# Taking the transposes of the large segments off TensorE in a fused Mamba-2 and feed-forward kernel

## The chip, the cores and the metric

The kernel runs as one program on one core of one Trainium2 chip. The metric is the time of one execution on the device, in microseconds (us). Smaller is better. The figure for a kernel is the median of its timed runs. Beside the timed runs there is one profiled execution, from which all durations of single instructions come.

## The reference, cut to what matters

The input `u` has 4 sequences of 1024 tokens with 256 features, in float32. One layer is computed: a Mamba-2 mixer, then a feed-forward block with 4-bit weights, each with a layer norm on its input, a layer norm on its output and a residual.

```python
x = u                                                    # (4, 1024, 256)
x = x + layernorm(mamba2(layernorm(x)))
x = x + layernorm(ffn(layernorm(x)))

def mamba2(u):
    z, xBC, dt = split(u @ in_proj)                      # 512 | 512+128+128 | 8
    xBC = silu(causal_conv1d(xBC))                       # 4 taps along the tokens
    x, B, C = split(xBC)                                 # 8 heads of 64 | 128 | 128
    dt = softplus(dt + dt_bias)
    # scan over the tokens of state[h] = exp(dt*A) * state[h] + B (x*dt), y = C . state + D*x
    y = scan(x, dt, A, B, C, D) * silu(z)
    y = y * rsqrt(mean(y*y) + EPS) * norm_weight
    return y @ out_proj                                  # 512 -> 256

def ffn(x):                                              # weights from 4-bit codes and block scales
    return (gelu(x @ Wg.T) * (x @ Wu.T)) @ Wd.T          # 256 -> 2048 -> 256
```

## The kernel before, in words

The 4096 tokens are cut into nine segments (`SEGS`): the first half of sequence 0 as two segments of 256 tokens (segments 0 and 1), and seven "large" segments of 512 tokens (segments 2 to 8). A large segment has four token blocks of 128. For every segment there is a mixer part (`mixer(s)`) and a feed-forward part (`ffn(s)`).

Matrix products contract over the partitions, so activations have to stand with features on the partitions ("by feature") for one product and with tokens on the partitions ("by token") for another. The kernel turns a tile with TensorE: a transpose is a product with the constant `ident`, 128 columns at a time, into a bank of PSUM, and ScalarE or VectorE then reads that bank. There are three such places:

- `norm_in`: the mixer's input `x` is normalised by token into `xn` (VectorE) and turned into `xnT` (two transposes for a token block, then a ScalarE copy for each half of the features).
- `inner(i)`: after the convolution, `xc` stands by feature. For each token block its four feature tiles of x are turned into the bank `px`, which VectorE reads twice (for `xdt` and `xw`), and the feature tile of B is turned into `pgb` and copied by ScalarE to `bt`. Five transposes for a token block.
- `turned(i)`: the normalised input of the feed-forward part, `xf`, is turned into `xfT`. Two transposes for a token block and one ScalarE copy.

The steps of a mixer are in this order: `norm_in`, `step_sizes` (dt), `features` and `convolve` for the six feature tiles, `decays`, then for the token blocks `inner`, `scan`, `gated`, `way_out` and `turned`, each a step behind the one before. From segment 4 on (`SEVEN`) and in the feed-forward of all large segments, a 2x2 block product is done with seven products instead of eight (`pair`, `seven`); the weights for it are fetched from DRAM (`stock`, `mstock`) into `wide` and `win` by SyncE's queue, and VectorE and ScalarE do additions and copies between the products. `widen_pair(j)` makes two of the 16 tiles of the hidden layer, and `narrow` multiplies by the last weight matrix into the banks `d`.

The program does not issue instructions as it is written. A `Recorder` takes down every instruction with its inputs, outputs and buffers, and `issue` then plays a list schedule: for each engine it picks, among what could start soonest, the step of lowest `rank`, and takes over the order found. A mixer of segment s has rank 10s - 10, the products of the feed-forward of segment s rank 25 + 10s and its last product rank 27 + 10s. So a mixer goes ahead of the feed-forward three segments before it. Costs of the plan are in `weigh`; for a DMA, `issue` takes 60 ns on SyncE's queue, then the bytes by a rate on one shared wire and 1700 ns to landing, and lets a consumer on another engine start `LATE_DMA` = 1500 ns after that. Each engine, SyncE's DMA queue among them, then runs its list strictly in order and waits where an input is not there. All instructions have the same line in the profile (L379, the place where the plan is written out), so they are told apart by tile names: `xn`, `xc` and `xf` with `ident` are transposes, `f` and `a` and `d` are banks of PSUM.

Buffers are handed out in the order of the recording, too. There are three `x`, two `xfT`, two `xf`, three `th`, one `xnT`, one `xc`, and two banks `a`. `big[0]` and `big[1]` hold the hidden layer of segments 0 and 1; later `big[0]` holds that of the large segments, and `big[1]` the gelu values of `widen_pair`.

Of the kernel before, what the change touches and what calls it, by code (L numbers as in the profile page):

```python
# [17 lines left out]
P = 128  # L18
# [18 lines left out]
SIDE = 2  # L37
OUT = True
SEVEN = 4
MASKED = -2.0 ** 100  # L40

ATANH = (2.000000007877749, 0.6666631593507933, 0.400248537235466, 0.2796141883358907,
# [126 lines left out]
class Recorder:  # L169
# [118 lines left out]
    def issue(self, tc, rank, patience):  # L288


        steps = self.steps
        follows = [[] for _ in steps]
        for st in steps:
            st.missing = len(st.before)
            st.ready = st.floor
            st.rank = rank(st)
            for b in st.before:
                follows[b.at].append(st)
        open_ = {e: [] for e in self.ENGINES.values()}
        table = "exp"  # L300
        for st in steps:
            if not st.missing:
                open_[st.engine].append(st)
        free = {e: 0.0 for e in open_}
        wires = 0.0
        bundle = None
        order = []
        while len(order) < len(steps):
            best = None
            for e, sts in open_.items():  # L310
                when = {}
                for st in sts:
                    starts = [b.pool.may_start(b) for b in st.buffers]
                    if None not in starts:
                        when[st] = max(starts + [st.ready, free[e]])
                if e == "ACT" and when:


                    now = min(when.values())
                    other = [st for st in when if st.table not in (None, table)]  # L320
                    for st in other:
                        when[st] += SWITCH
                    if len(other) < len(when):
# [12 lines left out]
            t, st = best  # L336
            e = st.engine
            st.start = t
            if e == "ACT" and st.table:
                table = st.table  # L340
            turn = min(PORT, max(0.0, free["POOL"] - t)) if st.port and t < EARLY else 0.0
            free[e] = t + st.busy + turn
            st.end = free[e] + st.after
            if st.name == "dma_start":
                if st.bytes > 20000:
                    wires = max(free[e], wires) + st.bytes / (230.0 if st.repeats else 350.0)
                    st.end = wires + 1700.0
# [12 lines left out]
            order.append(st)  # L360
            for f in follows[st.at]:
                flows = f.before[st]
                if e == "PE" and f.engine == "PE":
                    r = st.start
                elif f.engine != e:
                    r = st.end + slack(e, f.engine)
                elif flows:
                    r = st.end
                else:
                    r = st.start  # L370
                f.ready = max(f.ready, r)
                f.missing -= 1
                if not f.missing:
                    open_[f.engine].append(f)
        self.order = order
        with tc.manual_schedule():
            for st in order:
                real = lambda a: a.on(a.buf.pool.slots[a.buf.slot]) if isinstance(a, View) else a
                getattr(getattr(self.nc, st.queue), st.name)(  # L379
                    *[real(a) for a in st.args], **{k: real(a) for k, a in st.kwargs.items()})  # L380
# [25 lines left out]
def mamba_ffn_kernel(  # L406
    ctx: ExitStack,
    tc: tile.TileContext,
    u: bass.AP,
    w_in: bass.AP,  # L410
    conv_w: bass.AP,
    conv_b: bass.AP,
# [25 lines left out]
    def given(ap):  # L438
        return Pool([ap]).get()

    u, w_in, conv_w, conv_b, dt_bias, a_log, d_skip, norm_w, w_out = map(
        given, (u, w_in, conv_w, conv_b, dt_bias, a_log, d_skip, norm_w, w_out))
    g_pack, g_scale, u_pack, u_scale, d_pack, d_scale, out = map(
        given, (g_pack, g_scale, u_pack, u_scale, d_pack, d_scale, out))

# [12 lines left out]
        "rows": pool("rows", [CMAX * NH, P], 2, of=hbm), "dec": pool("dec", [P, 3 * CMAX * NH], 2),  # L458
# [8 lines left out]
    def get(tag):  # L467
        return pools[tag].get()
# [107 lines left out]
    tails = [fixed(f"tail{b}", [P, NF, 3]) for b in range(NB)]  # L576

    big = [fixed(f"big{j}", [P, 2 * MLP]) for j in range(2)]

    def over_heads(v, n):  # L580

# [2 lines left out]
    def little(tag, n):  # L584
        return get(tag)[:, :n]

    def rstd_of(var, n, factor=1.0):

        v = get("rsm")[:, :n]
        r.gpsimd.tensor_scalar(v, var, factor, EPS * factor, ALU.mult, ALU.add)  # L590
        r.gpsimd.tensor_tensor(v, v, mhalf[:, :n], ALU.pow)
        return v

    def stats_of(rows, who="m"):

# [140 lines left out]
    def mixer(s):  # L736
# [7 lines left out]
        def ps_a():  # L744
# [3 lines left out]
                return (banks_a if v_.get("out") else banks_f).get()  # L748
            return (banks_d if s == 1 and v_["n"] % 2 else banks_a).get()

        def norm_in():
            x = v_["x"] = xs[s]
            mv = stats_of([x[:, i, :] for i in range(NC)])
            rs = rstd_of(mv[:, :, 1], NC)
            xnT = v_["xnT"] = by_segment(s, "xnT", lambda t, c: t[:, :, c])
            pT = [ps_a() for kk in range(2)]
            for i in range(NC):
                xn = get("xn")
                r.vector.tensor_scalar(xn, x[:, i, :], mv[:, i, 0:1], rs[:, i : i + 1],
                                        ALU.subtract, ALU.mult)  # L760
# [108 lines left out]
        def convolve(f, pp):  # L869
# [25 lines left out]
            th = get("th")[:, :T]  # L895
            r.scalar.activation(th, h, AF.Tanh)
            r.vector.scalar_tensor_tensor(h, th, 1.0, h, ALU.add, ALU.mult)


        def inner(i):  # L900
# [30 lines left out]
                j = i * NH + h  # L931
                r.scalar.activation(e_[:, h, :], raw[h], AF.Exp, bias=v_["ncs"][:, j : j + 1])

            px = ps_a()
            for f in range(4):
                r.tensor.transpose(px[:, f * P : (f + 1) * P], xc[:, f, tok], ident)
            px = px.rearrange("p (h c) -> p h c", c=HD)
            xdt = v_["xdt", i] = get("xdt")
            r.vector.tensor_tensor(xdt, px, over_heads(v_["dt"][:, hs], HD), ALU.mult)
# [15 lines left out]
            pgb = ps_a()  # L955
            r.tensor.matmul(pgb[:, :P], lhsT=xc[:, 4, tok], rhs=xc[:, 5, tok],
                             start=True, stop=True)
            r.tensor.transpose(pgb[:, P : 2 * P], xc[:, 4, tok], ident)
            bt = v_["bt", i] = get("bt")
            r.scalar.copy(bt, pgb[:, P : 2 * P])  # L960
            r.vector.tensor_tensor(e_, e_, pgb[:, :P].unsqueeze(1).to_broadcast([P, NH, P]),
                                    ALU.mult)

# [109 lines left out]
        def way_out(i):  # L1073
# [7 lines left out]
            for c in range(4):  # L1081
# [55 lines left out]
    def ffn(s):  # L1137
# [237 lines left out]
```

## Time and profile before

| what | value |
|---|---|
| timed runs | 1000.05, 999.85, 998.04 us; median 999.85 |
| profiled execution, span from first to last instruction | 995.4 us |
| median less span | 4.45 us |
| TensorE busy | 983.0 us (99% of the span) |
| VectorE / ScalarE / GpSimd busy | 650.1 / 517.0 / 305.1 us |
| DMA packets, bytes | 48659, 111.76 MB |
| mean granted TensorE clock | 0.999 |

The profile gives the profiled execution's span and no further time of its own; the 4.45 us between it and the median of the timed runs lie outside the first and last instruction. In the profile PE is TensorE's matmul, PEld its loading of the stationary operand, DVE VectorE, ACT ScalarE, POOL GpSimd and SP (or SPq) SyncE's DMA queue. A group `a<-ident,xc` is an instruction that writes a bank `a` from `ident` and `xc`.

### The profile page before, as it was taken

The numbers are of one execution on the slowest core, as the hardware profiler recorded it, in microseconds if no ns is written. First come the engines' busy times: TensorE is split into PE (matmuls) and PEld (weight loads), VectorE is DVE, ScalarE is ACT, GpSimd is POOL, SyncE is SP. The second block draws the span as 40 slices with busy tenths as digits, with TensorE's granted clock in tenths as the row PEclk, the third lists the DMA queues.
The fourth block names the chain that finished last, engine by engine and source line by source line (L and its number), as shares of the span: only waits on it lengthen the run. The fifth ranks groups of instructions, "written<-read, shape, count | busy, mean of one in ns | idle before, by whom it ended". The sixth has DMA issues, their size and how long they took to land.

```text
span 995.4 us, 14948 instructions
## 1 busy us (share of the span) xinstructions
PE 983.0 (99%) x5275; PEld 813.7 (82%) x5275; DVE 650.1 (65%) x1412; ACT 517.0 (52%) x1289; POOL 305.1 (31%) x491
## 2 busy tenths in 40 slices
PE   8999999999999999999999999999999999999998
PEld 6788777877788878888888888888888888888886
DVE  4998576568666967787678754777467874432431
ACT  5645865447564764576457733576236762321321
POOL 2836654821250335024502431034310452001001
PEclk9999999999999999999999999999999999999999
DMA  6542153424423422354144423244233322422310
GB/s 203 110 112 91 78 167 117 170 64 139 163 76 98 131 81 92 127 159 156 43 145 142 157 75 106 91 136 153 76 116 132 98 102 96 148 74 95 107 43 21
DMA packets 48659, 111.76 MB, mean 112 GB/s; under 512 B 4664, under 2 KB 35768, under 8 KB 44472
## 3 DMA queue, kind: packets, MB, share of 16 engines
q1 hardware_dynamic: 48008, 110.78, 33.8%
q8 instruction: 41, 0.67, 0.3%
q14 instruction: 34, 0.28, 0.1%
q10 hardware_dynamic: 576, 0.02, 0.0%
HBM read 96.83 MB, written 13.96 MB: 111 GB/s over the span
## 4 chain that ended last, share of the span: by engine, by line
PE 94%; DVE 2%; POOL 1%; ACT 1%; issue 1%; POOLq 0%; DVEq 0%; ACTq 0%
PE f L379 48%; PE a L379 23%; PE d L379 23%; DVE xc L379 1%; DVE y L379 0%; DVE wide L379 0%; POOL sz L379 0%; ACT big L379 0%; DVE xn L379 0%; POOL y L379 0%; POOL rsf L379 0%; DVE yo L379 0%; POOL wd L379 0%; DVE e L379 0%; DVE big L379 0%
## 5 line engine op out<-in xcount | busy, mean ns | idle before, releaser
L379 PE MATMUL f<-wide 128*128 128x256 f32 x880 | 250.1, 382 | 0.1
L379 PE MATMUL f<-xfT,wide 128*128 128x256 f32 (+1 forms) x1024 | 248.4, 356 | 0.3 <-ACT big L379 0.2
L379 PE MATMUL d<-wd,big 128*128 128x256 f32 x992 | 248.0, 380 | 0.0
L379 PEld LDWEIGHTS d<-wd,big 128*128 128x128 f32 x992 | 183.6, 190 | 26.9 <-issue 4.1
L379 PEld LDWEIGHTS f<-xfT,wide 128*128 128x128 f32 x1024 | 171.2, 191 | 26.3 <-issue 5.9
L379 PEld LDWEIGHTS f<-wide 128*128 128x128 f32 x880 | 157.5, 190 | 32.2 <-issue 5.0
L379 DVE TENSOR_TENSOR f<-f,sums 128x256 f32<-128x256 f32 x216 | 92.4, 430 | 100.0 <-PE f L379 92.2
L379 POOL TENSOR_SCALAR_AFFINE_SELECT e<-e 128x1024 f32<-128x1024 f32 x31 | 35.3, 1137 | 201.5 <-DMA e<-rows 201.5
L379 ACT COPY f<-f 128x256 f32<-128x256 f32 x129 | 46.4, 362 | 93.0 <-PE f L379 70.4
L379 ACT ACTIVATE big<-f 128x512 f32<-128x512 f32 x108 | 63.1, 598 | 52.3 <-DVE f L379 40.8
L379 DVE TENSOR_TENSOR big<-big,f 128x512 f32<-128x512 f32 x108 | 73.2, 684 | 13.2 <-PE d L379 4.9
L379 ACT ACTIVATE e<-e,ncs 128x128 f32<-128x128 f32 x248 | 77.7, 392 | 5.2 <-POOL e L379 5.1
L379 DVE SCALAR_TENSOR_TENSOR xc<-f,cw,xc 128x511 f32<-128x511 f32 (+5 forms) x102 | 70.6, 713 | 1.8 <-ACT tail L379 0.4
L379 ACT ACT_TABLE_LOAD x52 | 66.7, 1283 | 4.3 <-issue 2.7
L379 PE MATMUL f<-xnT,win 128*128 128x256 f32 x240 | 66.1, 382 | 0.0
L379 POOL TENSOR_SCALAR rsf<-rsf 128x1 f32<-128x1 f32 x32 | 6.2, 193 | 187.1 <-ACT act L379 186.0
L379 PE MATMUL a<-wo,y 128*128 128x256 f32 x240 | 57.1, 381 | 0.0
L379 POOL TENSOR_TENSOR sz<-sz 128x256 f32<-128x256 f32 (+1 forms) x64 | 39.5, 619 | 35.5 <-ACT sz L379 34.2
L379 PEld LDWEIGHTS a<-wo,y 128*128 128x128 f32 x240 | 45.0, 190 | 6.3 <-DVE mvm L379 0.3
L379 PEld LDWEIGHTS f<-xnT,win 128*128 128x128 f32 x240 | 44.0, 190 | 7.2 <-ACT bt L379 0.8
L379 POOL TENSOR_TENSOR state<-state,dec 128x512 f32<-128x512 f32 x24 | 25.2, 1049 | 80.7 <-PE a L379 69.7
L379 DVE SCALAR_TENSOR_TENSOR fo<-d,rsf,x 128x256 f32<-128x256 f32 x30 | 14.3, 480 | 52.3 <-POOL rsf L379 52.2
(273 smaller groups left out, 1543.7 us busy)
## 6 DMA issues: line engine op xcount, KB each, us to landing
wide<-stock SPq DMA_DIRECT2D x28, 1792.0 KB, 7.3
e<-rows SPq DMA_DIRECT2D x31, 512.0 KB, 4.1
win<-mstock SPq DMA_DIRECT2D x25, 448.0 KB, 3.4
r<-rows SPq DMA_DIRECT2D x56, 128.0 KB, 4.6
stock<-sums SPq DMA_DIRECT2D x8, 512.0 KB, 2.6
out_dram<-fo SPq DMA_DIRECT2D x30, 128.0 KB, 1.7
x<-in_u_dram SPq DMA_DIRECT2D x7, 512.0 KB, 4.2
stock<-wide SPq DMA_DIRECT2D x6, 512.0 KB, 6.4
```

What stands on the lines that cost most here:

```text
L379: getattr(getattr(self.nc, st.queue), st.name)(*[real(a) for a in st.args], **{k: real(a) for k, a in st.kwargs.items()})
```

## The change

For the large segments the three turns are done without TensorE.

- **Mixer input** (segments 2 to 8): `xnT` is loaded by feature straight from a second copy of the input, `u_t`, which the host hands over transposed. The statistics stay by token. Mean and reciprocal deviation of the 512 tokens are stored to DRAM as one line each and loaded again with each line repeated over all partitions; GpSimd subtracts the one, VectorE multiplies by the other.
- **x and B** (segments 3 to 8, `TURNED`): `convolve` stores each of the five feature tiles to a DRAM tensor `planes`. For a token block four DMAs load 32x32 blocks of it in exchanged places into `blocked` (each for 32 partitions and 20 runs of 32 floats a partition), and one VectorE transpose of 128x640, which turns every 32x32 block in itself, finishes the turn in `by_rows`. `px` and `bt` are then parts of this tile in SBUF. Segments 0 to 2 keep their TensorE transposes here. `blocked` and `by_rows` lie in the upper half of `big[1]`, which also holds the hidden layer of segment 1.
- **Feed-forward input** (segments 2 to 8): `way_out` stores `xf` to DRAM (`halves`), `turned` loads it by four DMAs of 32x32 blocks (32 partitions, 8 runs of 32 floats each), and one VectorE transpose of 128x256 writes `xfT`.
- The planner counts a DMA whose runs are 32 long at 130 bytes/ns. `widen_pair` uses two places of `big[1]` for gelu values in turn instead of four.

```diff
@@ issue
-                    wires = max(free[e], wires) + st.bytes / (230.0 if st.repeats else 350.0)
+                    rate = 130.0 if st.shapes[0][-1] <= 32 else 230.0 if st.repeats else 350.0
+                    wires = max(free[e], wires) + st.bytes / rate
@@ pools
+        "planes": pool("planes", [5 * P, TMAX], 2, of=hbm),
+        "halves": pool("halves", [2, P, P], 2, of=hbm),
+        "lines": pool("lines", [2, CMAX * P], 2, of=hbm), ...
+    blocked = big[1][:, MLP : MLP + NX]
+    by_rows = [big[1][:, MLP + (k + 1) * NX : MLP + (k + 2) * NX] for k in range(2)]
@@ mixer
+        def norm_turned():
+            x = v_["x"] = xs[s]
+            r0, _ = rows_of(s)
+            mv = stats_of([x[:, i, :] for i in range(NC)])
+            rstd_of(mv[:, :, 1], NC, to=mv[:, :, 1])
+            xnT = v_["xnT"] = get("xnT")
+            r.sync.dma_start(out=xnT,
+                             in_=u_t[:, r0 : r0 + T].rearrange("(k p) t -> p k t", p=P))
+            lines = get("lines")
+            for k, op in enumerate((ALU.subtract, ALU.mult)):
+                r.sync.dma_start(out=lines[k].rearrange("(i p) -> p i", p=P), in_=mv[:, :, k])
+                by_token = get("th")
+                r.sync.dma_start(out=by_token, in_=lines[k].partition_broadcast(P))
+                (r.vector if k else r.gpsimd).tensor_tensor(
+                    xnT, xnT, by_token.unsqueeze(1).to_broadcast([P, 2, T]), op)
+
         def norm_in():
+            if s > 1:
+                return norm_turned()
@@ convolve
+            if s >= TURNED and f < 5:
+                if "planes" not in v_:
+                    v_["planes"] = get("planes")
+                r.sync.dma_start(out=v_["planes"][f * P : (f + 1) * P, :], in_=h)
@@ inner
-            px = ps_a()
-            for f in range(4):
-                r.tensor.transpose(px[:, f * P : (f + 1) * P], xc[:, f, tok], ident)
+            if s >= TURNED:
+                for c in range(4):
+                    at = i * P + 32 * c
+                    r.sync.dma_start(
+                        out=blocked[32 * c : 32 * c + 32, :].rearrange("p (g t) -> p g t", t=32),
+                        in_=v_["planes"][:, at : at + 32].rearrange("(g p) t -> p g t", p=32))
+                rows = by_rows[i % 2]
+                r.vector.transpose(rows, blocked)
+                px, bt = rows[:, : 4 * P], rows[:, 4 * P :]
+            else:
+                px = ps_a()
+                ...
-            r.tensor.transpose(pgb[:, P : 2 * P], xc[:, 4, tok], ident)
-            bt = v_["bt", i] = get("bt")
-            r.scalar.copy(bt, pgb[:, P : 2 * P])
+            if s < TURNED:
+                ...
+            v_["bt", i] = bt
@@ way_out
+            if s >= 2:
+                v_["halves", i] = get("halves")
+                r.sync.dma_start(out=v_["halves", i].rearrange("k t f -> t k f"), in_=xf)
@@ turned
+            if s >= 2:
+                halves, xf = v_["halves", i], get("xf")
+                for c in range(4):
+                    r.sync.dma_start(
+                        out=xf[32 * c : 32 * c + 32].rearrange("p k (g j) -> p (k g) j", j=32),
+                        in_=halves.rearrange("k t f -> (k t) f")[:, 32 * c : 32 * c + 32]
+                        .rearrange("(g p) j -> p g j", p=32))
+                r.vector.transpose(xfT[s][:, :, i * P : (i + 1) * P], xf)
+                return
@@ widen_pair
-            a = big[1][:, j % 4 * 2 * TMAX : (j % 4 + 1) * 2 * TMAX]
+            a = big[1][:, j % 2 * 2 * TMAX : (j % 2 + 1) * 2 * TMAX]
@@ kernel
+        ("u_t", g["L0_attn_u"].reshape(NB * L, DM).T),
```

More of the change, by code (lines that the diff above doesn't have):

```diff
@@ L39 @@
 SEVEN = 4
+TURNED = 3
+NX = 5 * P
 MASKED = -2.0 ** 100
@@ L409, in mamba_ffn_kernel @@
     u: bass.AP,
+    u_t: bass.AP,
     w_in: bass.AP,
@@ L439, in given @@
         return Pool([ap]).get()
-    u, w_in, conv_w, conv_b, dt_bias, a_log, d_skip, norm_w, w_out = map(
-        given, (u, w_in, conv_w, conv_b, dt_bias, a_log, d_skip, norm_w, w_out))
+    u, u_t, w_in, conv_w, conv_b, dt_bias, a_log, d_skip, norm_w, w_out = map(
+        given, (u, u_t, w_in, conv_w, conv_b, dt_bias, a_log, d_skip, norm_w, w_out))
     g_pack, g_scale, u_pack, u_scale, d_pack, d_scale, out = map(
@@ L457, in mamba_ffn_kernel @@
         "fo": pool("fo", [P, DM], 2), "cst": pool("cst", [CMAX * NH, P], 2),
-        "rows": pool("rows", [CMAX * NH, P], 2, of=hbm), "dec": pool("dec", [P, 3 * CMAX * NH], 2),
+        "rows": pool("rows", [CMAX * NH, P], 2, of=hbm),
+        "planes": pool("planes", [5 * P, TMAX], 2, of=hbm),
+        "halves": pool("halves", [2, P, P], 2, of=hbm),
+        "lines": pool("lines", [2, CMAX * P], 2, of=hbm), "dec": pool("dec", [P, 3 * CMAX * NH], 2),
         "edge": pool("edge", [P, NF, 3], 2), "part": pool("part", [P, NF, 3], 2),
@@ L585, in little, with rstd_of @@
         return get(tag)[:, :n]
-    def rstd_of(var, n, factor=1.0):
+    def rstd_of(var, n, factor=1.0, to=None):
         v = get("rsm")[:, :n]
+        to = to or v
         r.gpsimd.tensor_scalar(v, var, factor, EPS * factor, ALU.mult, ALU.add)
-        r.gpsimd.tensor_tensor(v, v, mhalf[:, :n], ALU.pow)
-        return v
+        r.gpsimd.tensor_tensor(to, v, mhalf[:, :n], ALU.pow)
+        return to
     def stats_of(rows, who="m"):
@@ L932, in inner @@
                 r.scalar.activation(e_[:, h, :], raw[h], AF.Exp, bias=v_["ncs"][:, j : j + 1])
-            px = ps_a()
-            for f in range(4):
-                r.tensor.transpose(px[:, f * P : (f + 1) * P], xc[:, f, tok], ident)
+            if s >= TURNED:
[9 more added lines that the diff above has]
+                px = ps_a()
+                for f in range(4):
+                    r.tensor.transpose(px[:, f * P : (f + 1) * P], xc[:, f, tok], ident)
             px = px.rearrange("p (h c) -> p h c", c=HD)
@@ L957, in inner @@
                              start=True, stop=True)
-            r.tensor.transpose(pgb[:, P : 2 * P], xc[:, 4, tok], ident)
-            bt = v_["bt", i] = get("bt")
-            r.scalar.copy(bt, pgb[:, P : 2 * P])
+            if s < TURNED:
+                r.tensor.transpose(pgb[:, P : 2 * P], xc[:, 4, tok], ident)
+                bt = get("bt")
+                r.scalar.copy(bt, pgb[:, P : 2 * P])
+            v_["bt", i] = bt
             r.vector.tensor_tensor(e_, e_, pgb[:, :P].unsqueeze(1).to_broadcast([P, NH, P]),
```

## The prediction

> **What bounds the kernel now.** I read the page first: its busy times, the 40 slices and the chain.
>
> ```profile
> PE 983.0 (99%) x5275; PEld 813.7 (82%) x5275; DVE 650.1 (65%) x1412; ACT 517.0 (52%) x1289; POOL 305.1 (31%) x491
> PE   8999999999999999999999999999999999999998
> DVE  4998576568666967787678754777467874432431
> PEclk9999999999999999999999999999999999999999
> PE 94%; DVE 2%; POOL 1%; ACT 1%; issue 1%; POOLq 0%; DVEq 0%; ACTq 0%
> ```
>
> TensorE has work in every slice at full clock, and 94% of the chain that ends last runs through it. It is idle for 995.4 - 983.0 = 12.4 us, and the windows put half of that (5.8 us) into the first 60 us. A busy TensorE could still hide waits, so I read the waits: its longest is 4.6 us, once, at the start, and no other is over 0.8 us. VectorE waits for TensorE (92.2 us before the additions of the seven products), not the other way. Work taken off TensorE therefore comes off the end, as long as nothing makes TensorE wait.
>
> Next, the groups with shapes kept apart, for the count of transposes, and the timeline for what one takes.
>
> ```profile
> L379 PE MATMUL a<-ident,xc 128*128 128x128 f32 x148 | 29.8, 275 | 0.1
> L379 PE MATMUL a<-ident,xf 128*128 128x128 f32 x62 | 11.9, 274 | 0.0
> L379 PE MATMUL a<-ident,xn 128*128 128x128 f32 x58 | 11.3, 275 | 0.3 <-DVE xn L379 0.3
> ```
>
> ```profile
> 800.52 0.60 PE L379 MATMUL a<-ident,xc 128*128 128x128 f32 x4
> 800.96 0.60 PE L379 MATMUL f<-xfT,wide 128*128 128x256 f32 x2
> ...
> 736.39 0.38 PE L379 MATMUL a<-ident,xn 128*128 128x128 f32 x2
> 736.61 0.60 PE L379 MATMUL f<-xfT,wide 128*128 128x256 f32 x2
> ```
>
> The 275 ns is the pass of one transpose through the pipeline. What TensorE gives up to it is the distance to the next start: four take 800.96 - 800.52 = 0.44 us, two take 0.22 us, so 0.11 us each.
>
> **What comes off TensorE.** Mixer input: 7 large segments x 4 blocks x 2 = 56 transposes. x and B: 6 segments x 4 x 5 = 120. Feed-forward input: 7 x 4 x 2 = 56. Together 232 x 0.11 = 25.5 us, all of it on the path.
>
> The row says 0.11 us between starts. The Trainium skill (TensorE: Matmul & The Clock Gate, Part 4: PE-mode transpose) gives about 275 ns for a transpose inside a kernel. The trace has that figure as a duration, and priced by it the saving would be 232 x 0.275 = 64 us (an estimate from that page) and the time 936 us. The spacing in the trace speaks against it, since the next product starts long before the 275 ns are over.
>
> **What comes off the other engines** counts nothing by itself: ScalarE loses 14 copies to `xnT` (590 ns), 24 to `bt` (266) and 28 to `xfT` (372), 25 us in all, and VectorE 28 of the `xn` steps (435 ns), 12 us. ScalarE is idle half the time, VectorE a third.
>
> **What VectorE and GpSimd get.** The trace has no VectorE transpose. Nearest rows by size: 128x256 in 430 ns (`f<-f,sums`), 128x512 in 764 (`y<-y,sz`, all SBUF), 128x1024 in 1216 (`e<-e,a`). I read 0.88 us for 640 columns and 0.43 for 256; at half the pace it would be 1.8 and 0.9. So 24 x 0.88 + 28 x 0.43 = 33 us, 7 multiplications of 1024 columns at 1.22 = 9 us, and `xdt` and `xw` from SBUF instead of PSUM 44 x 0.08 = 3 us: 45 us more, 12 less, VectorE near 683 us. Its 345 idle us cover that and, at half the pace, another 33. GpSimd gets 7 subtractions of 1024 columns, each twice `y<-xc,dsk` (1039 ns): 15 us, with 690 idle.
>
> **What SyncE's queue and the DMA engines get.** A segment from 3 on issues 5 stores of planes, 16 block loads, 4 stores and 16 loads of halves, 1 load of `xnT` and 4 for the lines: 46. Segment 2 issues 25. In all 6 x 46 + 25 = 301. A block load has 32 x 20 = 640 runs of 128 bytes, a load of halves 256. No row shows 128-byte runs. In the packet records of the trace a 96-byte packet takes 12 ns and a 512-byte one 27, so I take 13 and keep 27 as the other end. 90,112 such packets over 16 engines are 73 us (152 at the end), on top of 34% busy: with some 5 points for 21,760 longer packets 46 to 55%, no bound.
>
> What counts is when a turn is there, for the transpose stands in VectorE's list, in order, and behind it stand the additions and multiplications that TensorE's next products wait for. Rows for issue (timeline of SyncE's queue), landing (DMA issues of the page, the last number) and one tile:
>
> ```profile
> 72.75 4.81 SPq L379 DMA_DIRECT2D mstock<-win  x3
> 768.99 1.24 SPq L379 DMA_DIRECT2D r<-rows  x2
> ```
>
> ```profile
> wide<-stock SPq DMA_DIRECT2D x28, 1792.0 KB, 7.3
> e<-rows SPq DMA_DIRECT2D x31, 512.0 KB, 4.1
> ```
>
> ```profile
> L379 SPq DMA_DIRECT2D dtw<-in_w_in_dram x1: 469/469/469, 1.3 to 1.3; - x1
> ```
>
> One issue holds the queue 0.47 us (`dtw`, 256 runs of 32 bytes), 0.62 us (`r`, 256 runs of 512) or 1.60 us (`mstock<-win`, 640 runs of 512). The shortest landing of an `r` is 2.8 us after its issue began. So the last of four block loads lands 3 x 0.62 + 2.8 = 4.7 us after the first began; at the dear end 3 x 1.6 + 2.8 + 1.0 = 8.6.
>
> The plan lets VectorE have it after 4 x 81,920 / 130 = 2.5 us, 0.06, 1.7 and 1.5: 5.8 us. Its other rates stand up in the rows above (1,835,008 / 350 + 1,700 ns = 6.9 us for 7.3; 524,288 / 230 + 1,700 = 4.0 for 4.1), and 130 bytes/ns is 16 ns a packet and engine, between my two ends. For the halves the plan says 4 x 32,768 / 130 + 3,260 ns = 4.3 us, against 3 x 0.62 + 2.8 = 4.7. It counts 0.06 us an issue where the trace has 0.33 to 0.62, so other DMAs in the queue add to this. I take waits of 0.3 us on average for both kinds: 52 x 0.3 = 16 us of VectorE, of which half reaches TensorE, as VectorE has idle time to catch up in: 8 us. Ends: nothing, and 24 x 2.8 + 28 x 0.4 = 78 us (the rival below).
>
> The trace gives 12 ns for 96 bytes. The Trainium skill (DMA: Bandwidth & Descriptors, Specifications) puts line rate at 512 bytes and more, so a 128-byte run would cost nearly what 512 bytes cost. By that rule a block's 2560 packets at 27 ns would need 4.3 us, land 0.7 us late, and add 5 us (estimates): 989 us. No run here shows 128-byte runs yet.
>
> **What the longer way costs the chain of a mixer.** Planes must land (2.6 us, as `stock<-sums`), then 4.7 us of loads and 0.9 of transpose: 8 us before the first `xdt`. On the other side the norm (397.2 to 405.7 us in segment 5, 8.5 us) no longer needs a bank `a` and can run beside the mixer before. Mixers now start 98 us apart where they are close, from 103 to 735 us. The next segment's feed-forward needs the result only a feed-forward later, and seven mixers could each grow by 14 us, to 112, before segment 8 came late. Cost nothing; if the cover is gone, 7 us for each us per mixer beyond 14.
>
> One place has no cover, the first large segment:
>
> ```profile
> 205.46 0.38 PE L379 MATMUL a<-ident,xf 128*128 128x128 f32 x2
> 205.68 0.60 PE L379 MATMUL d<-wd,big 128*128 128x256 f32 x2
> 206.11 0.59 PE L379 MATMUL f<-xfT,wide 128*128 128x256 f32 x2
> 206.28 0.76 DVE L379 TENSOR_TENSOR wide<-xfT 128x256 f32<-128x256 f32 x2 [1.64 <-ACT xfT L379]
> ```
>
> The feed-forward of segment 2 starts right behind its last transpose. The last `xf` is there at 204.6 us; store (2.1), loads (4.7) and transpose (0.4) make 211.8 instead of 206.2. TensorE has the end of segment 1 and the dt and first features of segment 3 for those 5.6 us; I charge 2 us (0 to 6). Two places for gelu values instead of four: reused two pairs later, nothing.
>
> **The sum.** The profiled execution: 995.4 - 25.5 + 8 + 2 = 979.9 us of span. The timed median lies 4.45 us above the span: 984.3 us. Without any stall it is 974, and a few of the 12.4 idle us might go as well: 971. A measurement of this kernel can tell about 0.2% (2 us) from no change.
>
> **Rivals.**
> 1. *VectorE stands before the transposes* (slower). Loads at the dear pace come 2.8 us (blocks) and 0.4 us (halves) after the plan: 78 us of VectorE. Half reaching TensorE gives 999.85 - 25.5 + 2 + 39 = 1015 us, all of it 1054. It decides from 23.5 us at TensorE on, 0.45 us a turn. For it: TensorE takes each product the moment its addition is done, so it has little lead; the planner's 60 ns an issue is too low. Against: `mstock<-win` ran in a burst behind 1.5 MB of other stores, and ScalarE waits only 0.8 us in all for `r`, planned by the same rule.
> 2. *The mixers become the chain.* One tile `blocked` means that a block's loads wait for the transpose before. If each block took its own 4.7 + 0.9 us in line, a mixer grew by 4 x 5.6 less what the 10 us between blocks hide; at 18 us, 4 beyond the cover, 28 us are lost: 974 + 28 = 1002 us. Against: blocks are 10 us apart now.
> 3. *The transposes cost TensorE nothing*, hidden beside weight loads: 999.85 plus the 10 us: 1010 us. The 0.22 us between starts speaks against it.
>
> **Chances.** Forecast 0.63 (own range 971 to 996), rival 1 0.24, rival 2 0.10 (a third of it still faster or the same), rival 3 0.03. Faster by over 0.2%: 0.63 + 0.02 = 0.65; within 0.2%: 0.05; slower: 0.30. The range goes from 971 up to 1020, which takes in rival 2 and 3 and over half of rival 1.
>
> **What would show it.** Right: TensorE 5043 matmuls, near 957 us busy and 98% of the span; VectorE 1443 instructions, near 683 us; about 165,000 DMA packets (48,659 as now, 90,112 and 21,760 more, 301 x 16 semaphore writes); waits of VectorE for `blocked` and `xf` loads under 20 us; a small gap before segment 2's feed-forward. Wrong: long rows of VectorE waiting for a DMA with TensorE waiting for VectorE behind them (rival 1); TensorE idle in stretches after 850 us (rival 2); TensorE's busy time unchanged (rival 3).

## The result, and the profile after

The changed kernel takes **1069.36 us** (median of 4 runs, 1067.99 to 1072.15) against 999.89 us for the kernel before on the same chip: ratio 1.0702 [1.0682, 1.0722], 7% slower. The forecast was 984.3 us, its range ended at 1020. The profiled execution took 1072.15 us, with a span of 1070.4 us: 75.0 us more than the 995.4 us before.

The page first: busy times, slices and the chain.

```profile
PE 991.0 (93%) x5043; PEld 808.7 (76%) x5043; DVE 687.9 (64%) x1443; ACT 500.5 (47%) x1227; POOL 325.6 (30%) x498
PE   8999999859987999599969999879998999999998
PEclk8989999979997999899989999989999999999999
PE 33%; DMA 4%; DVE 2%; issue 1%; SPq 0%; POOL 0%; POOLq 0%; ACT 0%; DVEq 0%; ACTq 0%
```

TensorE runs 232 matmuls fewer, as the change says, and yet is busy for longer: 991.0 us against 983.0. It is idle for 1070.4 - 991.0 = 79.4 us against 12.4. The slices under 9 do not lie at random: their low points are slices 9, 13, 17, 21, 27 and 31, some 4 to 6 slices (107 to 160 us) apart, about the pace at which mixers start, and the granted clock shows 7 or 8 tenths in the first five of them. So the 75.0 us are 67.0 us more idle, less 25.5 us of transposes, and 33.5 us by which what is left runs slower (957.5 us expected, 991.0 found).

The waits of three engines show who is late. The columns are: who waits, for what; total us, how often, the longest. First SyncE's DMA queue, then VectorE, then TensorE.

```profile
SPq L382 <- DMA lines<-mvm: 83.0, 12, 11.3
```

```profile
DVE xf L382 <- DMA halves<-xf: 42.9, 7, 17.9
DVE xfT L382 <- DMA xf<-halves: 23.7, 7, 6.3
DVE xnT L382 <- DMA th<-lines: 16.8, 4, 12.8
DVE big L382 <- DMA big<-planes: 0.5, 1, 0.5
```

```profile
PE f L382 <- DVE f L382: 37.3, 12, 8.7
PE a L382 <- DVE xnT L382: 18.8, 2, 13.2
```

VectorE stands for 42.9 + 23.7 + 16.8 = 83.4 us for DMAs of the change, and TensorE behind it. But the transposes for x and B (`big<-planes`), which were the prediction's main worry, wait for 0.5 us in all. Among the DMAs, what the queue itself waits for most is a store of 2 KB, the line of 512 means or deviations. The DMA issues of the page say why (KB each, median us from issue to landing):

```profile
lines<-mvm SPq DMA_DIRECT2D x14, 2.0 KB, 8.7
big<-planes SPq DMA_DIRECT2D x96, 80.0 KB, 4.0
```

The small store lands after 8.7 us, later than the 1.8 MB of `wide<-stock` (7.3 us, as before): it writes 512 values to 512 places of 4 bytes. Its load `th<-lines` needs it, so the queue, in order, stands until it has landed, and everything listed behind stands too. The timeline of SyncE's queue at segment 3 (start and length in us), and of VectorE and TensorE in the same stretch:

```profile
195.99 0.79 SPq L382 DMA_DIRECT2D lines<-mvm  x1
208.03 0.33 SPq L382 DMA_DIRECT2D th<-lines  x1
208.46 0.39 SPq L382 DMA_DIRECT2D lines<-mvm  x1
216.21 0.33 SPq L382 DMA_DIRECT2D th<-lines  x1
216.63 0.39 SPq L382 DMA_DIRECT2D halves<-xf  x1
217.07 1.96 SPq L382 DMA_DIRECT2D xf<-halves  x4
```

```profile
221.14 0.41 DVE L382 TENSOR_SCALAR xf<-x,mvm,rsm 128x256 f32<-128x256 f32 x1 [17.90 <-DMA halves<-xf]
```

```profile
202.70 6.85 PE L382 MATMUL d<-wd,big 128*128 128x256 f32 x31
222.74 1.08 PE L382 MATMUL a<-xnT,dtw 128*32 128x128 f32 x16 [13.19 <-DVE xnT L382]
```

Two line stores hold the queue from 196 to 216 us. The store `halves<-xf`, which belongs to the feed-forward of another segment, goes out only at 216.63; VectorE cannot overwrite that `xf` before, and stands for 17.90 us. Behind that in VectorE's list is the multiplication that finishes `xnT`. TensorE has nothing left after 209.55 us and starts again at 222.74. A window of the stretch after that gap (columns: stretch, its length, busy us of PE, PEld, DVE, ACT and POOL with counts, granted clock, DMA share, GB/s):

```profile
223.00:230.00 7.00, 7.00 (x31) 3.77 (x24) 2.69 (x7) 1.69 (x4) 0.00 (x0) 0.75 0.45 102
```

TensorE is busy throughout, but at a mean clock of 0.75: the clock records show half clock for 13.7 us from 212.9 us on, and 11 such stretches in the run, 82 us together; in the profiled execution of before there is none but after the last matmul. Nine of the eleven begin during or behind idle time, which is how idle time also makes the busy time grow. The other two, at 18 and 56 us and 17 us long together, have at most 0.15 us of idle time in the 10 us ahead of them. In all TensorE is busy for 56 us of the 82. Had each matmul there taken twice its time, that would be 28 us (an estimate), so the clock can be most of the 33.5 us and not all of it.

### The profile page after: what moved, and what is told of

It is laid out like the page before. It is cut to its first block, busy times and chain, and to the rows that moved or that the text cites. A ratio compares the mean times of both kernels' runs of the same rounds, so it can differ in the third digit from the quotient of the medians.

```text
span 1070.4 us, 15002 instructions
## 1 busy us (share of the span) xinstructions
PE 991.0 (93%) x5043; PEld 808.7 (76%) x5043; DVE 687.9 (64%) x1443; ACT 500.5 (47%) x1227; POOL 325.6 (30%) x498
## 2 busy tenths in 40 slices
DMA packets 165350, 142.23 MB, mean 133 GB/s; under 512 B 106760, under 2 KB 145032, under 8 KB 161160
## 5 line engine op out<-in xcount | busy, mean ns | idle before, releaser
L382 PE MATMUL f<-wide 128*128 128x256 f32 x880 | 262.1, 396 | 40.2 <-DVE f L382 36.5
L382 PE MATMUL f<-xfT,wide 128*128 128x256 f32 (+1 forms) x1024 | 256.3, 363 | 4.5 <-DMA wide<-stock 3.8
L382 PE MATMUL d<-wd,big 128*128 128x256 f32 x992 | 245.4, 383 | 0.0
L382 PEld LDWEIGHTS f<-wide 128*128 128x128 f32 x880 | 163.0, 196 | 83.9 <-DVE f L382 46.0
L382 PEld LDWEIGHTS d<-wd,big 128*128 128x128 f32 x992 | 187.6, 191 | 30.5 <-issue 6.3
L382 PEld LDWEIGHTS f<-xfT,wide 128*128 128x128 f32 x1024 | 179.2, 196 | 33.9 <-issue 10.6
L382 ACT ACTIVATE e<-e,ncs 128x128 f32<-128x128 f32 x248 | 77.7, 390 | 10.3 <-POOL e L382 10.2
L382 PE MATMUL f<-xnT,win 128*128 128x256 f32 x240 | 69.3, 396 | 0.5 <-issue 0.4
L382 PEld LDWEIGHTS f<-xnT,win 128*128 128x128 f32 x240 | 46.2, 199 | 9.2 <-issue 1.7
L382 ACT ACTIVATE sz<-y 128x512 f32<-128x512 f32 x32 | 20.1, 629 | 64.3 <-DVE y L382 64.2
L382 POOL TENSOR_TENSOR y<-xc,dsk 128x512 f32<-128x512 f32 x32 | 32.9, 1039 | 55.5 <-DVE xc L382 25.6
```

What stands on the lines that cost most here:

```text
L382: getattr(getattr(self.nc, st.queue), st.name)(*[real(a) for a in st.args], **{k: real(a) for k, a in st.kwargs.items()})
```

## The experiments

**The theories.** A: the line stores land late and hold SyncE's queue (the place and price of the prediction's rival 1, with another cause). B: the traffic of the two block turns, 90,112 packets of 128 bytes, slows loads and VectorE. C: the list schedule found a worse order; any change of the list moves the time.

### Undo one turn, keep one turn

`e1_norm_pe` puts only the mixer's input back on TensorE (the two other turns stay), `e2_norm_only` does the reverse.

```diff
@@ norm_in (e1)
-            if s > 1:
-                return norm_turned()
```
```diff
@@ (e2)
-TURNED = 3
+TURNED = 9
@@ way_out, turned
-            if s >= 2:
+            if s >= 9:
```

> Undoes one part: the mixer input is normalised and turned on TensorE as before (56 transposes come back, 6.2 us); x, B and the feed-forward input stay off TensorE. Theory L (the 4-byte line stores hold SyncE's queue, each 8 to 12 us until it lands, 83 us in all, and everything queued behind comes late): no line stores, so VectorE's waits for DMA fall from 83 to under 20 us, TensorE's idle time from 79 to about 20 us, the clock back to 0.99, and the time is 999.9 - 176 x 0.11 + 5 = 985 us (975 to 995). Rival W (the long way of halves and planes through DRAM, with VectorE standing before it, is the cost whatever the lines do): the 67 us before halves<-xf and xf<-halves stay, time 1040 us or more.

> Does one part alone: only the mixer input is turned without TensorE; x, B and the feed-forward input are turned on TensorE as before. Theory L: the line stores still hold SyncE's queue some 80 us, but no halves or planes wait behind them, only weight blocks, rows and outputs; slower than before, 1005 to 1035 us, with waits for th<-lines on GpSimd and VectorE. Rival W: nothing of its cause is left, 56 x 0.11 = 6 us saved: 994 us.

Measured: e1 **1012.38 us**, ratio 1.0112 [1.0083, 1.0142]; e2 **1089.49 us**, 1.0894 [1.0867, 1.0921]. The page of e1, and the waits of SyncE's queue in e2:

```profile
PE 980.9 (97%) x5099; PEld 802.7 (79%) x5099; DVE 684.7 (68%) x1464; ACT 515.1 (51%) x1247; POOL 313.8 (31%) x491
```

```profile
SPq L382 <- DMA lines<-mvm: 105.3, 12, 12.9
```

Theory A had put e1 at 975 to 995 us and e2 at 1005 to 1035, the rival (the long way through DRAM itself) e1 at 1040 or more and e2 at 994. The rival is out. Both runs are slower than A expected, too, and by e1 the lines are not the whole loss. Without the lines 57 of the 69 us are gone: idle 31.4 us instead of 79.4, clock 0.989 instead of 0.961, VectorE's waits for DMAs of the change 8.6 us instead of 83.4. With the lines alone, and none of the 128-byte packets, all of the loss and more is there. Against B. The direct path shows in e2: TensorE's dt product waits 58.2 us for `xnT` in 6 places, up to 15.4 us each. But e1 is still 12.8 us slower than before, although it has 176 transposes (176 x 0.11 = 19.4 us) less. The long waits are gone; what is left is idle time in pieces of at most 3.7 us, 31.4 us in all against 12.4, and 17 us of busy time over the 983.0 - 19.4 us that one would expect. Half clock, 20 us of it in this run, can be at most 10 of these 17.

### The same lines in longer runs, and a plan that knows their price

`e3_run16` keeps all three turns and stores each line in another order: the four values of a partition stand side by side, 128 runs of 16 bytes instead of 512 of 4. GpSimd and VectorE then read the repeated line with a stride. `e4_plan8` leaves the kernel's work as it is and tells the plan what a line store costs.

```diff
@@ norm_turned (e3)
+            each = get("rsm")[:, :NC], rstd_of(mv[:, :, 1], NC)
+            r.gpsimd.tensor_scalar(each[0], mv[:, :, 0], 1.0, 0.0, ALU.mult, ALU.add)
-                r.sync.dma_start(out=lines[k].rearrange("(i p) -> p i", p=P), in_=mv[:, :, k])
+                r.sync.dma_start(out=lines[k].rearrange("(p i) -> p i", p=P), in_=each[k])
-                    xnT, xnT, by_token.unsqueeze(1).to_broadcast([P, 2, T]), op)
+                    ..., by_token.rearrange("q (p i) -> q i p", p=P).unsqueeze(1)..., op)
```
```diff
@@ issue (e4), line stores alone
-                    st.end = free[e] + 1900.0
+                    st.end = free[e] + 8000.0
```

> The changed kernel with one size changed: mean and reciprocal deviation are stored in the order (token in the block, block), 128 runs of 16 bytes instead of 512 runs of 4 bytes; the loads are the same, GpSimd and VectorE read the repeated line in steps of 16 bytes. Theory L with the size of the runs as its cause: the store lands in 2 to 3 us instead of 8, near the 1.9 us of the plan, and the time is 975 to 990 us. Theory L with the wait itself as its cause (a store to DRAM that SyncE's queue has to wait out, whatever its runs): landing stays above 6 us and the time above 1040 us. Rival W: landing shorter, time still above 1040 us.

> The changed kernel with one number of the plan changed: a line store is counted at 8.0 us to landing instead of 1.9; the instructions are the same, their order on the engines differs. If the plan's wrong figure is what turns the slow store into a stall (other DMAs were put behind the wait because the plan thought it over), the time falls to 980 to 1000 us with the landing still at 8 us. If the slow store costs by itself, as the chain of the mixers grows by two of them, 1040 us or more. Rival W: as now, 1060 us.

Measured: e3 **1008.02 us**, 1.0089 [1.006, 1.0117]; e4 **1053.33 us**, 1.0525 [1.0503, 1.0547]. The DMA issues of e3:

```profile
lines<-rsm SPq DMA_DIRECT2D x14, 2.0 KB, 2.8
```

The same 2 KB, the same queue, the same turns: the store lands in 2.8 us instead of 8.7, and 61 us come back, more than two orders of one kernel differ by anywhere below (27 us at most). That is A, with the price of 4-byte runs as its root. It is one order of each kernel, though. Over the orders tried here and below, the kernel with 16-byte runs takes 1008 to 1030 us and the one with 4-byte runs 1053 and 1069, so the runs of 4 bytes cost between 24 and 61 us.

e4 shows that the plan's ignorance is the smaller part: with 8 us counted, the order changes and 16 us come back, but the store still lands in 10.2 us, and 53 us stay. It also shows a second way from the slow store to TensorE. One line of the queue's waits, then the stretch at segment 3 on SyncE's queue, VectorE and TensorE:

```profile
SPq L383 <- DMA lines<-mvm: 1.3, 1, 1.3
```

```profile
192.19 3.54 SPq L383 DMA_DIRECT2D lines<-mvm  x2
196.41 1.13 SPq L383 DMA_DIRECT2D halves<-xf  x1
207.09 0.41 DVE L383 TENSOR_SCALAR xf<-x,mvm,rsm 128x256 f32<-128x256 f32 x1 [8.36 <-DMA halves<-xf]
213.29 2.08 PE L383 MATMUL f<-xfT,wide 128*128 128x256 f32 x4 [6.27 <-DVE xfT L383]
```

The queue now stands for the lines for 1.3 us in all instead of 83.0, because the plan puts other DMAs between a line store and its load. But these land late as well. The store `halves<-xf`, issued at 196.41 behind two line stores, is done at 207.0, 10.6 us later, against a median of 2.0 in the run. VectorE stands 8.36 us for it and TensorE 6.27 us behind VectorE. The loads `xf<-halves` that follow a line store within 9 us land after 9.2 us in the median (13 whose landing is known), the others after 1.9; with 16-byte lines (e3) both kinds take 1.9. So the slow store delays what is issued behind it even where the queue does not wait. How much of the loss went which of the two ways no run separates.

### The store by itself

`m1_stores` leaves out the whole computation. It stores small tiles to DRAM one after the other on a queue that has nothing else, four times each.

> Leaves out the whole computation (the output is zeros) and measures stores to DRAM one at a time, four times each, on an otherwise idle queue: 512 runs of 4 bytes scattered as the lines are, the same 512 values to neighbouring places, 128 runs of 4 bytes, 128 of 16, 128 of 32, 128 of 512. If the number of 4-byte writes to scattered places is the price: 6 to 8 us for the first, 2 to 3 us for all others. If short runs as such are slow: the 4, 16 and 32 byte ones all above 4 us, 512 bytes below 2. If it was the company in the queue (weights being fetched at the same time): all near 2 us.

One execution of 207.32 us. Its DMA issues:

```profile
four<-mv SPq DMA_DIRECT2D x4, 2.0 KB, 8.8
one<-mv SPq DMA_DIRECT2D x4, 0.5 KB, 7.6
sixteen<-mv SPq DMA_DIRECT2D x4, 2.0 KB, 1.4
five<-wide SPq DMA_DIRECT2D x4, 64.0 KB, 1.5
...
packed<-mv SPq DMA_DIRECT2D x4, 2.0 KB, 7.3
```

`four` is the kernel's store, 512 places of 4 bytes: 8.8 us with nothing beside it, so contention is not the reason. `packed` writes the same 512 values to neighbouring places, still one by one: 7.3. `one` is 128 values of 4 bytes: 7.6. With 16 bytes a place (`sixteen`), 32 (`thirty`, also 1.4 us) or 512 (`five`): 1.4 to 1.5. So it is the store of single 4-byte values that costs 6 to 7 us more. Their number (four times as many cost 1.2 us) and whether they lie apart (1.5 us) matter less. In `four`, `packed` and `one` the values are read singly as well as written singly, and no run separates the two. None of the three outcomes expected of this run fits as it stands: not the number of scattered writes, not short runs as such, not the company in the queue. The Trainium skill (DMA: Bandwidth & Descriptors, Specifications) puts the limit for line rate at 512 bytes and names a read-modify-write below it. In landing time the runs here show no loss at 16 and 32 bytes, and a large one at 4.

### Where the rest went: the order

e1 and e3 have 176 and 232 transposes less and no long wait left, but both stand 1% above the kernel before. A second set changes numbers of the plan only, which give another order of the same work. First, 450 ns instead of 60 for each issue on SyncE's queue (`weigh`), which is nearer to the trace, in e1 (`f1`), e3 (`f2`), the kernel before (`g1`) and e1 without the feed-forward turn (`g2`); and e1's two turns one at a time (`f3` the feed-forward input alone, `f4` x and B alone). `g3` is `f1` with 100 ns more in the plan for a VectorE transpose.

```diff
@@ weigh (f1, f2, g1, g2)
-        return 60.0, 0.0
+        return 450.0, 0.0
@@ (f3: e1 and TURNED)
-TURNED = 3
+TURNED = 9
@@ way_out, turned (f4, g2: e1 and this)
-            if s >= 2:
+            if s >= 9:
```

> The first experiment (mixer input on TensorE, x, B and feed-forward input off it, 1012 us) with one number of the plan changed: an issue on SyncE's queue is counted at 450 ns instead of 60. Same instructions, another order. Theory I (what is left over is SyncE's queue running behind a plan that thinks an issue nearly free: x loads, outputs and halves come late and VectorE stands before them): 985 to 1000 us, TensorE's waits for VectorE under 15 us, clock 0.995. Rival D (VectorE has 35 us more to do, in stretches where it was nearly full, and its additions come late by themselves): 1005 us or more, with the same waits of TensorE for VectorE. If neither, the order alone moves it by a few us either way.

> The kernel with lines stored in runs of 16 bytes (all three turns off TensorE, 1008 us) with an issue on SyncE's queue counted at 450 ns in the plan instead of 60. Theory I: 980 to 998 us, under the kernel before. Rival D: 1003 us or more.

> Only the feed-forward input is turned without TensorE (56 transposes fewer, 6.2 us); mixer input, x and B are turned on TensorE. Prices what is left of the first experiment (1012 us, where 19.4 us of transposes are saved and 32 lost). If the halves carry it (store, load and transpose inside one mixer step, two tiles xf for twice the uses): 1005 to 1020 us. If the planes carry it: 993 to 1000 us.

> Only x and B of segments 3 to 8 are turned without TensorE (120 transposes fewer, 13.2 us); mixer input and feed-forward input are turned on TensorE. If the planes carry the loss that is left (16 block loads and 5 stores a segment, 24 transposes of 835 ns on VectorE): 1000 to 1015 us. If the halves carry it: 985 to 993 us, faster than the kernel before.

> The kernel before with the one number of the plan changed that brought 15.7 us in the kernel with x, B and the feed-forward input off TensorE (an issue on SyncE's queue counted at 450 ns instead of 60). Same instructions, another order. Theory I (the wrong price hurts only where the queue is full of new issues): the kernel before has 230 issues in 995 us and room, so 997 to 1002 us. Rival P (any other order of this plan moves the kernel by as much, the 15.7 us were luck): outside 990 to 1008 us. If the new price alone is worth some us here too, 985 to 996 us, and then the gain of the kernel with 996.7 us is not due to the turns.

> Only x and B off TensorE (1003.0 us), with an issue on SyncE's queue counted at 450 ns in the plan. 120 transposes less are 13.2 us. Theory I: 987 to 996 us, faster than the kernel before. Rival D (VectorE's 24 transposes and what they push aside are the cost): 1000 us or more.

> The version that came in at 996.7 us, with the plan told also what a VectorE transpose takes (835 and 438 ns measured, 737 and 334 in the plan: 100 ns more each). If the plan's picture of VectorE is what is left of the loss: 985 to 994 us. If not: 995 to 1002 us.

| kernel | turns off TensorE | median us | ratio to before [95%] |
|---|---|---|---|
| f1 | x and B, feed-forward; 450 ns | 996.66 | 0.9968 [0.9951, 0.9984] |
| f2 | all three, 16-byte lines; 450 ns | 1023.30 | 1.0218 [1.018, 1.0257] |
| f3 | feed-forward alone | 1009.52 | 1.0089 [1.0062, 1.0115] |
| f4 | x and B alone | 1002.97 | 1.0041 [1.0023, 1.0059] |
| g1 | none (before); 450 ns | 1011.64 | 1.0131 [1.0105, 1.0157] |
| g2 | x and B alone; 450 ns | 1010.17 | 1.0108 [1.0085, 1.0131] |
| g3 | as f1, transpose 100 ns dearer in the plan | 1005.40 | 1.0065 [1.0046, 1.0085] |

For f1 alone one could say that an honest price of the issue is what was missing. g1 speaks against that: the same number makes the kernel before, which has none of the new DMAs, 12 us slower; it makes f2 15 us slower than e3, and g3 loses 9 us to a mere 100 ns in the plan. In each of these the order is another one. f1 beats both kernels: its TensorE is busy for 973.3 us of a span of 994.6, idle for 21.3, with a mean clock of 0.997. Its lead of 0.3% is well inside what the order alone does.

The last set was to measure that spread with numbers that have nothing to do with DMAs: the plan's time from an instruction to its consumer on another engine (`LATE`), and the slack within which the plan prefers rank to an early start (`PATIENCE`), each in the kernel before (`p0`), e1 (`p1`) and e3 (`p3`).

```diff
@@ (p0, p1, p3 _late130)
-LATE_PE, LATE, LATE_DMA = 75.0, 100.0, 1500.0
+LATE_PE, LATE, LATE_DMA = 75.0, 130.0, 1500.0
@@ (p0, p1, p3 _wait60)
-PATIENCE = 30.0
+PATIENCE = 60.0
```

> The kernel before with a neutral number of the plan moved (the slack it leaves between two engines 130 ns instead of 100): same instructions, another order. Theory O (the order of the kernel before is an unusually good one, and any new order costs some 10 us, so that part of the changed kernel's loss is not due to the turns): 1003 to 1015 us, as the 1011.6 us with the other price of an issue. If orders are alike: 997 to 1002 us, and that 1011.6 us came from the 450 ns itself.

> x, B and feed-forward input off TensorE, mixer input on it (1012.4 us), with the same neutral number moved (130 instead of 100 ns). Theory O: somewhere in 990 to 1015 us, and below the kernel before under the same plan by some of the 19.4 us of transposes that are saved. Rival (the turns through DRAM cost what they save): as slow as the kernel before under the same plan, or slower.

> All three turns off TensorE, lines in runs of 16 bytes (1008.0 us), with the same neutral number moved. Theory O: 990 to 1020 us, below the kernel before under the same plan by some of the 25.5 us. Rival: not below it.

> The kernel before with another neutral number of the plan moved (how long it lets an engine wait for a step of better rank: 60 ns instead of 30). Theory O (the order of the kernel before is unusually good): 1003 to 1015 us. If orders are alike: 997 to 1002 us.

> x, B and feed-forward input off TensorE, mixer input on it, with the same number moved (60 instead of 30 ns). Theory O: 985 to 1012 us, below the kernel before under the same plan. Rival (the turns through DRAM cost what they save): not below it.

> All three turns off TensorE, lines in runs of 16 bytes, with the same number moved. Theory O: 985 to 1020 us, below the kernel before under the same plan. Rival: not below it.

All medians in us, one column for each order:

| kernel | as written | issue 450 ns | LATE 130 | PATIENCE 60 | mean |
|---|---|---|---|---|---|
| before | 999.9 | 1011.6 | 1026.4 | 1012.0 | 1012.5 |
| x, B and feed-forward off TensorE (e1) | 1012.4 | 996.7 | 1000.3 | 1013.0 | 1005.6 |
| all three, 16-byte lines (e3) | 1008.0 | 1023.3 | 1029.8 | 1022.6 | 1020.9 |

The order alone moves each kernel by 16 to 27 us, and the kernel before happens to have the best of its four. Single comparisons at 1% therefore say nothing about the turns. Over four orders the two block turns give 6.9 us of the 19.4 us that their transposes cost, and the third turn, even with 16-byte lines, loses 15.3 us against e1. With four values each and such a spread (e1 is slower than before under two of the four orders, e3 faster than e1 under one), both are tendencies and not shown. Where the third turn would lose its time is open. One place shows in `f2`, where TensorE stands 8.65 us up to 219 us for `xnT`, the same product as above, at the end of the chain of statistics, store, load, subtraction and multiplication.

## Why the prediction was wrong, point by point

**The step that failed: the line stores had a count and no price.** "1 load of `xnT` and 4 for the lines" went into the number of issues and packets, and neither the 8.7 us to landing nor what is issued behind them had a term in the sum. The prediction asked of each block load when it lands and who stands behind it, but not of these four DMAs, and the plan's flat 1.9 us for small DMAs was not questioned. Its term for VectorE's waits, "52 x 0.3 = 16 us of VectorE, ... 8 us", was a fair size for the block turns by themselves: without the lines, in e1, VectorE waits 8.6 us for them. In the changed kernel `big<-planes` is 0.5 us, but `xf<-halves` is 23.7 and `halves<-xf` 42.9. The last is a store, and the prediction had no term for a store that keeps VectorE from the next `xf`. The missing term is the difference that e3 shows, 1069.4 - 1008.0 = 61 us, and by the other orders of both kernels at least 24. The trace of before has no store of single values; its nearest row, a small store of longer runs (`rows<-cst`, 16 KB, 1.4 us), would not have shown the price either, so the term needed a wide upper end.

**The mixer's chain was taken to "cost nothing".** The norm no longer needs a bank `a`, that is so, but it needed SyncE's queue twice in a row, and that was shared with the `halves` of another segment's feed-forward. The seam of segment 2, priced at 2 us, was the only place where a late turn was thought to have no cover; in e2 the dt product waits for `xnT` in six places, in the changed kernel in two (18.8 us).

**The clock was no term.** Idle was counted as idle only. The mean clock went from 0.999 to 0.961, and what TensorE still had to do took 33.5 us longer, a third of the 67.0 + 33.5 us that were lost. At most some 28 us of it are half clock (the estimate above); what the rest is, no run shows.

**The order was taken as given.** Even with the lines mended, 974 to 984 us was not reached by any of four orders (1008.0 to 1029.8). That every change of the list gives another order, worth 16 to 27 us between four, had no term. Of the 85 us between forecast and result, 24 are still there in e3 (1008.0 against 984.3). The order can make that much, but that it does is not shown.

**What held.** Matmuls, VectorE's instructions and GpSimd's as counted (5043, 1443, 498), DMA packets 165,350 for "about 165,000", VectorE busy 687.9 us for 683. The groups with shapes kept apart give the transposes and the subtraction (count, then busy us and mean ns):

```profile
L382 DVE STREAM_TRANSPOSE big<-big 128x640 f32<-128x640 f32 x24 | 20.1, 836 | 0.6 <-DMA big<-planes 0.5
L382 POOL TENSOR_TENSOR xnT<-xnT,th 128x1024 f32<-128x1024 f32 x7 | 16.4, 2346 | 35.8 <-DMA th<-lines 35.8
L382 DVE STREAM_TRANSPOSE xfT<-xf 128x256 f32<-128x256 f32 x28 | 12.3, 439 | 23.8 <-DMA xf<-halves 23.7
```

836 and 439 ns for the 0.88 and 0.43 us read from the nearest rows, so rows of the same size were a good guide; 2346 ns for a subtraction on GpSimd priced at twice 1039; 13.6 ns for a 128-byte packet, for 13. The 0.11 us of a transpose: with each start-to-start distance on TensorE set to the median of its shape in before, the whole list sums to 952.5 us before and 926.8 after, 25.7 us less for the 25.5 claimed, and in e3, at a clock of 0.992, TensorE is busy for 970.0 us instead of 983.0. Rival 3 is out by that; rival 2 by the 0.5 us of `big<-planes`, and because TensorE is busy for 215.2 of the 220 us after 850. Rival 1 had the place (VectorE stands for DMAs, TensorE behind it) and, at 78 us, nearly the size of the wait (83.4), with the wrong DMA as its cause; e2 shows that by having none of those loads. That the sizes are alike is chance. Its 1015 to 1054 us still fell short, and it too had no term for the clock.

## What to carry to other kernels

Price every DMA that a change adds, the 2 KB ones too, from issue to landing, and name who is queued or in flight behind it: here 14 stores of 28 KB together cost between 24 and 61 us, and the 90,112 packets of 128 bytes 8.6 us of VectorE's waits once the lines were gone. Don't write single 4-byte values to DRAM on a queue that others use; put four side by side and read them back with a stride. And where a list schedule sets the order, compare a change over several orders before a per cent or two is put down to it.

## What the runs showed of the hardware

A store of 4-byte values to DRAM takes 7.3 to 8.8 us to land on an idle queue, one of 16 to 512 bytes a place 1.4 to 1.5 us.

A DMA issued behind such a store lands late too: in e4 9.2 us in the median for `xf<-halves` within 9 us behind a line store, 1.9 us otherwise.

TensorE's clock can fall to half after a gap under 2 us, and the length of the gap alone does not decide it. First f2, then e3 (one line of TensorE's timeline and one window each; the value behind the five engines of a window is the clock):

```profile
763.46 0.64 PE L382 MATMUL a<-xnT,dtw 128*32 128x128 f32 x16 [1.75 <-DVE xnT L382]
764.00:769.00 5.00, 5.00 (x20) 3.83 (x17) 3.11 (x10) 0.89 (x3) 0.00 (x0) 0.66 0.61 257
```

```profile
218.73 1.13 PE L382 MATMUL f<-wide 128*128 128x256 f32 x4 [3.63 <-DVE wide L382]
219.00:226.00 7.00, 7.00 (x27) 4.73 (x27) 6.90 (x23) 2.78 (x8) 0.00 (x0) 1.00 0.35 94
```

In f2 an idle time of 1.75 us is followed by a clock of 0.66 in the mean for 5 us, which is half clock for 3.4 us; a pair of 128x256 products takes 1.06 us there and 0.59 after it. In e3 an idle time of 3.63 us is followed by full clock. The Trainium skill (TensorE: Matmul & The Clock Gate, Why this matters for your kernels) warns of idle gaps over some 3 us; by these runs 1.75 us was enough once and 3.63 us was not, and the measurement decides. What decides between them no run here was made to show.
